# Self-attention and involution on one core: exponentials summed by transposed reductions over pairs of key tiles, three rotating banks of tap weights, and a finer end of the last image

## The chip, the cores and the metric

The kernel runs on one core of one Trainium2 chip. The metric is the device time of one execution in microseconds (us). All data are float32. The engines are TensorE (PE, matmuls; PEld its weight loads), VectorE (DVE), ScalarE (ACT), GpSimd (POOL) and SyncE (SP), whose queue issues nearly all DMAs.

## The reference

The input x has 4 images of 512 channels and 64 x 64 pixels (n = 4096). Two layers follow one another.

```
q, k, v = wq x + bq, wk x + bk, wv x + bv          # 128 channels each
attn    = softmax(q^T k)                           # 4096 x 4096 per image
y       = wo (v attn^T) + bo + x                   # 512 channels

o1  = relu(s1 * (W1 y) + b1)                       # 128 channels
w   = Ws relu(sr * (Wr o1) + br) + bs              # 8 groups x 49 taps per pixel
inv[g,c,h,w] = sum over the 7 x 7 taps of w[g,tap,h,w] * o1_padded[g,c,h+i,w+j]
out = s3 * (W3 inv) + b3 + y
```

The 16 channels of a group share the 49 weights of a pixel.

## The kernel before

The whole program is written out in Python, so that the order in which a function emits instructions is the order on each engine. `fast_path` does the work; a slower `general_path` follows only if a test of the softmax sums fails.

**Attention.** For each image `keys_values` makes the keys `kt` and the values `vT` for 4096 positions. `attention` then goes through 8 blocks of 512 queries (a block is a chunk of 8 image rows); the last block of the last image is cut into two of 256 queries. A block has 32 steps, one for each tile of 128 keys: `score` multiplies keys and queries (`pss`), ACT takes the exponential into `pt` (L665), and PE multiplies it by the values into the bank `po`. Scores run two steps ahead. A block of 256 queries puts two key tiles into one step, so it has 16 steps. The sum of the exponentials over the keys is kept beside it: at each step DVE adds `pt` to an accumulator `pacc` in PSUM (L694 copies the first, L696 adds, L699 adds the last into `sums`). `ptpool` has five buffers, `ps_s` two.

**The end of a block.** `finish_block` is a generator: `chores`, called in each step, advances it a little, so that its matmuls lie between those of the next block. It reduces `sums` in 32 x 32 transposed blocks (L537), adds the four partition groups up by a matmul (`pl`), takes the reciprocal, spreads it, scales `on`, projects (`pwo`, added to x at L560), makes o1 (`p`), writes it to DRAM (`pix`, padded) and makes the reduced channels `red` for the weights. Only one such generator advances at a time.

**Involution.** A unit is 4 image rows (`UR`), so an image has 16 units and a chunk two. A unit holds two tiles (`NT`) of 2 rows x 64 columns = 128 pixels, with pixels on partitions. `weights` multiplies `red` into the taps' weights `pw` of both tiles, in two PSUM banks. `ring` keeps 12 rows (`RING`) of o1 as windows of 7 columns; `pump` loads them from `pix` as rows get written and as older ones come free. For each of the 7 columns x and for two groups of row offsets (`DYS`: 4 and 3), one DVE multiplication (L356) covers both tiles: 4 x 2 x 128 = 1024 elements for the first group, 768 for the second. Where the 12-row ring wraps within a group, each is cut into pieces of 512 and 512, or 512 and 256. Four product buffers (`prods`) lie between DVE and POOL, which adds the products into `acc` (L380) and at the end of the unit adds its four rows up (L389).

The involution is emitted by `pace`, a planner inside `chores`: an instruction is emitted when enough PE time has passed (`TAPS_A_US`), its rows are expected in the ring, and the planned backlog of DVE and POOL is under a few us. A new unit first waits for its predecessor's last planned DVE instruction:

```
yield from until(free["dve"] + 0.3)
pw = early.pop((b, u), None) or weights(b, u)
```

**The tail.** After the last attention matmul the list `tail` is filled and the planner no longer waits: a loop takes one step of `finishing`, one of `closing` and one of the taps in turn. Every second product is then added by PE (`pa`, a matmul with the identity) and not by POOL. `closing` holds `turn_unit`, which brings a unit's sums into channel order, and `close_chunk`, which multiplies by W3 (`py`), adds (L461) and stores. The last chunk closes in two halves of 256 pixels.

PSUM has eight banks: two for `ps`, one each for `po` and `pacc` (tag "acc"), two for `pw` and two for `ps_s`. After the attention the two of `ps_s` go to a second buffer of `pw`.

Of the kernel before, what the change touches and what calls it, by code (L numbers as in the profile page):

```python
# [15 lines left out]
P = 128  # L16
# [44 lines left out]
DYS = (0, 4), (4, 3)  # L61
TAPS_A_US = 1.56

# [4 lines left out]
DVE_OP, POOL_OP = 0.7, 1.28  # L68
# [15 lines left out]
def fast_path(  # L84
# [28 lines left out]
    ptpool = pool("pt", 5)  # L113
# [12 lines left out]
    wpools, early = [ps1], {}  # L126
# [16 lines left out]
    okr = const.tile([P, 1], F32, name="okr")  # L143

# [70 lines left out]
    def v1(i):  # L215
        return vec[:, i : i + 1]
# [23 lines left out]
    def pump():  # L240

        nonlocal load
        while load // STEP in written:
            b, row = divmod(load, STEP)
            rows, us = written[b]

            end = H + SR - UR if rows == H else rows + PAD - 1
            n = min(b * STEP + end, low + RING) - load
            n = min(n, RING - load % RING, PIECE if b == B - 1 else RING)
            if n <= 0:  # L250
                break
            for h in range(2):
                src = pix[b % 2][row + h : row + h + n, :W, :]
                windows = bass.AP(
                    tensor=src.tensor, offset=src.offset, ap=[[P, W], [WP * P, n], [1, K * P]]
                )
                nc.sync.dma_start(
                    ring[h * W : (h + 1) * W, load % RING : load % RING + n]
                    .rearrange("p r x c -> p r (x c)"),
                    windows,  # L260
                )
            free["dma"] = max(free["dma"], us)
            us = takes("dma", ROW_US * n) + LAND_US
            landing.update((load + i, us) for i in range(n))
            load += n
            if row + n == H + SR - UR:
                load = (b + 1) * STEP
# [7 lines left out]
    def weights(b, u):  # L275
        red, col = reds[b, u]
        wpools.append(wpools.pop(0))
        pw = wpools[0].tile([P, NT, CH], F32, tag="w", name=f"pw_{b}_{u}")
        for t in range(NT):

            rows = slice(t * (P // NT), t * (P // NT) + CR + 1)
            pixels = slice(col, col + P)
            mm(
                pw[:, t, : NTAP * G], red[rows, pixels], wt[rows, O_WT : O_WT + NTAP * G],
                shared=2,
            )
        return pw
# [17 lines left out]

    def involution():
        nonlocal low, due
        while True:
            while not units:
                yield "none"  # L310
            b, u = units.pop(0)
            acc = work2.tile([P, NT, 4, P], F32, tag="acc", name=f"acc_{b}_{u}")
            yield from until(free["dve"] + 0.3)
            pw = early.pop((b, u), None) or weights(b, u)
            begin = pe + 0.5
            pa, ops = None, []
            base = b * STEP + u * UR
            for dy0, n in DYS:

                at = (base + dy0) % RING  # L320
                whole = at + n + NT < RING + 1
                pieces = [(dy0, n)] if whole else [(dy0, 2), (dy0 + 2, n - 2)]
                ops += [(x, dy, k) for x in range(K) for dy, k in pieces]
            for o, (x, dy, n) in enumerate(ops):
                if o and dy >= DYS[1][0] > ops[o - 1][1]:
                    low = base + UR
                    pump()
                    if tail and units:
                        early[units[0]] = weights(*units[0])
                rows = [(base + dy + t * 2) % RING for t in range(NT)]  # L330
                while base + dy + n + NT > load:
                    yield "wait"
                landed = max(landing[base + dy + i] for i in range(n + NT))
# [6 lines left out]
                free["pool"] = max(free["pool"], takes("dve", DVE_TAPS[0] + DVE_TAPS[1] * n))  # L340
                takes("pool", POOL_TAPS[0] + POOL_TAPS[1] * n)
                due -= n
                d0 = dy - DYS[dy >= DYS[1][0]][0]
                first = x == 0 and dy < DYS[1][0]
                prod, p0 = acc, d0
                if not first:
                    prod, p0 = prods.tile(
                        [P, NT, 4, P], F32, tag="prod", name=f"prod_{b}_{u}_{o}"
                    ), 0
                col = (x * K + dy) * G  # L350
                lines = ring[:, rows[0] : rows[0] + n, x, :]
                image = bass.AP(
                    tensor=lines.tensor, offset=lines.offset,
                    ap=[lines.ap[0], [(rows[1] - rows[0]) * K * P, NT], [K * P, n], [1, P]],
                )
                product = nc.vector.tensor_tensor(  # L356
                    prod[:, :, p0 : p0 + n, :].rearrange("p t d (g c) -> p t d g c", g=G),
                    image.rearrange("p t d (g c) -> p t d g c", g=G),
                    pw[:, :, col : col + n * G].unsqueeze(3)
                    .broadcast_to([P, NT, n * G, GC])  # L360
                    .rearrange("p t (d g) c -> p t d g c", d=n),
                    ALU.mult,
                )
                if not tail:
                    tc.keep_in_program_order(product)
                if first:
                    pass
                elif tail and o % 2:

                    begun = pa is not None  # L370
                    if not begun:
                        pa = ps1.tile([P, NT, P], F32, tag=("po", "acc")[u % 2], name=f"pa_{b}_{u}")
                    for t in range(NT):
                        for d in range(n):
                            mm(
                                pa[:, t, :], prod[:, t, d, :], ident,
                                not begun and t == d == 0, False,
                            )
                else:
                    nc.gpsimd.tensor_tensor(  # L380
                        acc[:, :, d0 : d0 + n, :], acc[:, :, d0 : d0 + n, :], prod[:, :, :n, :],
                        ALU.add,
                    )
# [89 lines left out]
    def keys_values(b):  # L473
# [3 lines left out]
        for i, c in enumerate(KEYS):  # L477
# [20 lines left out]
            pv = ps1.tile([P, 4, P], F32, tag=("po", "acc")[i % 2], name=f"pv_{b}_{c}")  # L498
# [21 lines left out]
    def finish_block(b, c, off, n, po, sums):  # L520
# [5 lines left out]
        def pause(us, steps):  # L526
# [11 lines left out]
            blocks, sums.rearrange("p (k q) -> p k q", q=TB), AX.X, ALU.add, apply_transpose=True  # L538
# [3 lines left out]
        for i in range(CH // n):  # L542
            mm(pl, quads, blocks[:, i * n // TB : (i + 1) * n // TB], i == 0, i == CH // n - 1)
# [77 lines left out]
        pr = ps.tile([P, CH // NT], F32, tag="mm", name=f"pr_{name}")[:, : n // NT]  # L621
        for t in range(NT):
            half = slice(t * (P // NT), (t + 1) * (P // NT))
            mm(
                pr[half], w_slice(O_WP, 0)[:, half],
                o1.rearrange("p (u t x) -> p u t x", t=NT, x=P)[:, :, t, :], shared=2,
            )
        red = redpool.tile([P, CH // NT], F32, tag="red", name=f"red_{name}")[:, : n // NT]
        nc.scalar.activation(red, pr, AF.Relu, bias=v1(V_BP), scale=v1(V_SP))
        for i in range(tiles // NT):  # L630
            reds[b, top // UR + i] = red, i * P
# [15 lines left out]
    def attention(b, kt, vT, q):  # L647
        blocks = [(c, 0, CH) for c in range(NCH)]
        if b == B - 1:

            blocks[-1:] = [(NCH - 1, off, CH // 2) for off in (0, CH // 2)]

        steps = [(k, j) for k, (_, _, n) in enumerate(blocks) for j in range(N // P * n // CH)]
        qs, pts, pos, paccs = {}, {}, {}, {}
        qs[0] = q

        def score(m):
# [6 lines left out]
            pt = ptpool.tile([P, CH], F32, tag="pt", name=f"pt_{b}_{k}_{j}")  # L664
            nc.scalar.activation(pt, pss, AF.Exp)  # L665
            pts[m] = pt
# [3 lines left out]
        for m, (k, j) in enumerate(steps):  # L670
            c, off, n = blocks[k]
            nj = N // P * n // CH
            if j == 0:
                pos[k] = ps1.tile([P, CH], F32, tag="po", name=f"po_{b}_{k}")[:, :n]
                paccs[k] = ps1.tile([P, CH], F32, tag="acc", name=f"pacc_{b}_{k}")
# [9 lines left out]
            pt = pts.pop(m)  # L685
# [6 lines left out]
            takes("dve", DVE_OP)  # L692
            if j == 0:
                nc.vector.tensor_copy(paccs[k], pt)  # L694
            elif j < nj - 1:
                nc.vector.tensor_tensor(paccs[k], paccs[k], pt, ALU.add)  # L696
            else:
                sums = work1.tile([P, CH], F32, tag="sums", name=f"sums_{b}_{k}")
                nc.vector.tensor_tensor(sums, paccs.pop(k), pt, ALU.add)  # L699
                f = finish_block(b, c, off, n, pos.pop(k), sums)  # L700
                next(f)
                finishing.append(f)
# [17 lines left out]
    wpools.insert(0, pool("ps_w", 1, space=bass.MemoryType.PSUM, reuse_waits="tile"))  # L720
    wpools.reverse()
# [403 lines left out]
```

## Time and profile before

| what | value |
|---|---|
| timed runs, median (lowest to highest of 3) | 2607.41 us (2604.98 to 2607.64) |
| profiled execution, first to last instruction | 2605.7 us |
| median less the span | 1.7 us |
| PE busy | 2587.9 us (99%), granted clock 0.997 |
| DVE busy | 1874.2 us (72%) |
| POOL busy | 1823.5 us (70%) |
| ACT busy | 835.8 us (32%) |
| DMA | 244 MB, 38.6% of 16 engines' span |

The profile was taken in one execution; it gives no time of its own beside the span, so the 1.7 us stand for what lies around it. A "busy" time is the union of an engine's instructions. "Idle before" is the time in which an engine had nothing running before the instructions of that group, and the arrow names what ended it. In a timeline a row is a run of like instructions: start, length, engine, line, operation, tile written and tiles read, shape, count. In the window view a row gives each engine's busy time in that stretch with its number of instructions, then the granted clock of PE, the share of the DMA engines and GB/s. The attention's last matmul starts near 2526 us; the last tap product ends at 2593.3 us.

### The profile page before, as it was taken

The numbers are of one execution on the slowest core, as the hardware profiler recorded it, in microseconds if no ns is written. First come the engines' busy times: TensorE is split into PE (matmuls) and PEld (weight loads), VectorE is DVE, ScalarE is ACT, GpSimd is POOL, SyncE is SP. The second block draws the span as 40 slices with busy tenths as digits, with TensorE's granted clock in tenths as the row PEclk, the third lists the DMA queues.
The fourth block names the chain that finished last, engine by engine and source line by source line (L and its number), as shares of the span: only waits on it lengthen the run. The fifth ranks groups of instructions, "written<-read, shape, count | busy, mean of one in ns | idle before, by whom it ended". The sixth has DMA issues, their size and how long they took to land.

```text
span 2605.7 us, 24569 instructions
## 1 busy us (share of the span) xinstructions
PE 2587.9 (99%) x7484; PEld 1246.5 (48%) x7484; DVE 1874.2 (72%) x2677; ACT 835.8 (32%) x1378; POOL 1823.5 (70%) x1197
## 2 busy tenths in 40 slices
PE   9999999999999999999999999999999999999998
PEld 7444444445544444444644444444464444444577
DVE  0447777877575787788676678788757678777887
ACT  1333333332233333333223333333323333333330
POOL 0007788877881788887885468888788577877886
PEclk9999999999999999999999999999999999999999
DMA  6033232445615344233651434443463433222343
GB/s 236 1 75 63 55 85 73 99 99 150 164 43 112 63 101 95 61 84 82 180 129 45 103 69 101 101 92 74 118 171 83 101 93 93 72 60 58 73 91 102
DMA packets 208798, 244.33 MB, mean 94 GB/s; under 512 B 109640, under 2 KB 128528, under 8 KB 208528
## 3 DMA queue, kind: packets, MB, share of 16 engines
q1 hardware_dynamic: 208224, 242.31, 38.6%
q8 instruction: 61, 1.00, 0.2%
q14 instruction: 81, 0.66, 0.1%
q10 hardware_dynamic: 432, 0.36, 0.0%
HBM read 193.57 MB, written 49.06 MB: 93 GB/s over the span
## 4 chain that ended last, share of the span: by engine, by line
PE 91%; POOL 4%; DVE 3%; issue 1%; DMA 0%; ACT 0%; SPq 0%; POOLq 0%; DVEq 0%; ACTq 0%
PE pss L220 32%; PE po L220 31%; PE pv L220 4%; PE pk L220 4%; PE pq L220 4%; PE pwo L220 4%; PE py L220 4%; PE p L220 4%; POOL acc L380 4%; PE pw L220 2%; DVE prod L356 1%; PE pa L220 1%; DVE pacc L696 1%; PE pr L220 1%; POOL acc L389 0%
## 5 line engine op out<-in xcount | busy, mean ns | idle before, releaser
L380 POOL TENSOR_TENSOR acc<-acc,prod 128x768 f32<-128x768 f32 (+3 forms) x1063 | 1701.5, 1620 | 760.5 <-DVE prod L356 712.4
L220 PE MATMUL pss<-q,k 128*128 128x512 f32 (+1 forms) x2112 | 1056.3, 585 | 0.0
L220 PE MATMUL po<-pt,v 128*128 128x512 f32 (+1 forms) x2112 | 1047.7, 581 | 0.0
L665 ACT ACTIVATE pt<-pss 128x512 f32<-128x512 f32 x1024 | 611.3, 597 | 1252.0 <-PE pss L220 1184.9
L356 DVE TENSOR_TENSOR prod<-ring,pw 128x512 f32<-128x512 f32 (+3 forms) x1092 | 886.7, 847 | 44.6 <-POOL acc L380 41.7
L696 DVE TENSOR_TENSOR pacc<-pacc,pt 128x512 f32<-128x512 f32 x958 | 664.6, 694 | 243.2 <-ACT pt L665 216.2
L220 PEld LDWEIGHTS po<-pt,v 128*128 128x128 f32 x2112 | 399.3, 190 | 482.2 <-issue 462.2
L220 PEld LDWEIGHTS pss<-q,k 128*128 128x128 f32 x2112 | 391.9, 190 | 466.2 <-issue 459.3
L404 DVE STREAM_TRANSPOSE turned<-acc 128x256 f32<-128x256 f32 x48 | 21.4, 446 | 217.4 <-POOL acc L389 217.4
L220 PE MATMUL py<-accT,wt 128*128 128x512 f32 (+1 forms) x264 | 132.3, 584 | 4.0 <-DVE x L461 3.3
L220 PE MATMUL pwo<-on,wt 128*128 128x512 f32 (+1 forms) x264 | 130.3, 586 | 0.0
L220 PEld LDWEIGHTS pv<-wt,x 128*128 128x128 f32 x1024 | 119.6, 192 | 15.3 <-issue 15.0
L389 POOL TENSOR_TENSOR acc<-acc 128x512 f32<-128x512 f32 x120 | 119.5, 996 | 9.4
L461 DVE SCALAR_TENSOR_TENSOR x<-py,vec,x 128x512 f32<-128x512 f32 (+1 forms) x132 | 95.7, 726 | 36.1 <-PE py L220 35.8
L220 PE MATMUL pv<-wt,x 128*128 128x128 f32 x1024 | 120.2, 275 | 0.0
L220 PE MATMUL p<-x,wt 128*128 128x512 f32 (+1 forms) x264 | 119.2, 579 | 0.0
L578 ACT ACTIVATE x<-x,vec 128x512 f32<-128x512 f32 (+1 forms) x132 | 92.9, 706 | 80.0 <-PE p L220 74.9
L220 PE MATMUL pk<-x,wt 128*128 128x512 f32 x256 | 117.3, 596 | 0.1
L220 PE MATMUL pq<-x,wt 128*128 128x512 f32 (+1 forms) x264 | 115.4, 580 | 0.0
L560 DVE SCALAR_TENSOR_TENSOR x<-pwo,bo,x 128x512 f32<-128x512 f32 (+1 forms) x132 | 95.2, 727 | 22.8 <-PE pwo L220 21.7
L356 DVE TENSOR_TENSOR acc<-ring,pw 128x1024 f32<-128x1024 f32 (+1 forms) x84 | 78.7, 955 | 17.6 <-PE pw L220 17.6
L220 PEld LDWEIGHTS pq<-x,wt 128*128 128x128 f32 x264 | 50.0, 190 | 60.2 <-issue 56.7
(57 smaller groups left out, 733.6 us busy)
## 6 DMA issues: line engine op xcount, KB each, us to landing
x<-x_dram SPq DMA_DIRECT2D x55, 1024.0 KB, 5.7
ring<-pix SPq DMA_DIRECT2D x74, 448.0 KB, 8.3
ring<-pix SPq DMA_DIRECT2D x24, 1344.0 KB, 9.7
out_dram<-x SPq DMA_DIRECT2D x31, 1024.0 KB, 4.2
ring<-pix SPq DMA_DIRECT2D x24, 896.0 KB, 10.7
ring<-pix SPq DMA_DIRECT2D x30, 672.0 KB, 10.2
ring<-pix SPq DMA_DIRECT2D x6, 2240.0 KB, 19.5
pix<-o1t SPq DMA_DIRECT2D x192, 32.0 KB, 1.7
```

The source lines that it names most:

```text
L220: return nc.tensor.matmul(o, lhsT=lhsT, rhs=rhs, start=start, stop=stop)
L356: product = nc.vector.tensor_tensor(prod[:, :, p0 : p0 + n, :].rearrange("p t d (g c) -> p t d g c", g=G), image.rearrange("p t d (g c) -> ...
L380: nc.gpsimd.tensor_tensor(acc[:, :, d0 : d0 + n, :], acc[:, :, d0 : d0 + n, :], prod[:, :, :n, :], ALU.add,)
L389: nc.gpsimd.tensor_tensor(acc[:, :, :n, :], acc[:, :, :n, :], acc[:, :, n : 2 * n, :], ALU.add)
L404: nc.vector.transpose(blocks.rearrange("p (t k q) -> p t k q", t=NT, q=TB), acc[:, :, 0, :].rearrange("p t (k q) -> p t k q", q=TB),)
L461: nc.vector.scalar_tensor_tensor(xt[:, t, :], py, v1(V_S3 + t), xt[:, t, :], ALU.mult, ALU.add)
L560: nc.vector.scalar_tensor_tensor(xt[:, t, :], pw, bo[:, t : t + 1], xt[:, t, :], ALU.add, ALU.add)
L578: nc.scalar.activation(xt[:, t, :], xt[:, t, :], AF.Identity, bias=v1(V_B3 + t))
L665: nc.scalar.activation(pt, pss, AF.Exp)
L696: nc.vector.tensor_tensor(paccs[k], paccs[k], pt, ALU.add)
```

## The change

Five things are done at once.

1. `pt` holds a pair of key tiles (three buffers of 2 x 512 and not five of 512). After each second step DVE reduces the pair with a transposed `tensor_reduce` to 32 numbers per partition in `sums`; `finish_block` then adds those up over the pairs with one strided reduction. `pacc` and its PSUM bank go, and `pv` has one bank.
2. The tap weights lie in three PSUM banks that rotate by tile (`taps_w`, `slots`). A unit's second row group is done one tile after the other. While the second tile is done, the next unit's weights are made in the bank that is free and in the one that the first tile has left.
3. The products of a unit's second group have 384 elements and not 768 (or 256 and 128 where the ring wraps, which is now only in the second tile).
4. The last block of the last image is 256, 128 and 128 queries. Its last two units are done in the parts that `LAST` lists (unit, tiles, first row offset, number of offsets), in an order in which some parts of both need no row of the last 128 queries. Two padded rows (`PADDED`) are neither loaded nor multiplied.
5. In the tail the sums on PE (`pa`) have two banks of their own, and weights need none.

```diff
-    ptpool = pool("pt", 5)
+    ptpool = pool("pt", 3)
...
+    taps_w = ps1.tile([P, WSLOTS, CH], F32, tag="w", name="taps_w")
...
+PADDED = 2
+LAST = (
+    (0, (0, 1), 0, 2), (0, (0, 1), 2, 2),
+    (0, (0, 1), 4, 2), (0, (0,), 6, 1), (1, (0,), 0, 4),
+    (0, (1,), 6, 1), (1, (1,), 0, 4), (1, (0, 1), 4, 1), (1, (0,), 5, 2),
+)
...
+    def slots(b, u):
+        first = (b * NU + u) * NT
+        return [(first + t) % WSLOTS for t in range(NT)]
...
-    def weights(b, u):
-        red, col = reds[b, u]
-        wpools.append(wpools.pop(0))
-        pw = wpools[0].tile([P, NT, CH], F32, tag="w", name=f"pw_{b}_{u}")
-        for t in range(NT):
+    def weights(b, u, tiles=range(NT)):
+        for t in tiles:
+            red, col = reds[b, u * NT + t]
+            slot = slots(b, u)[t]
             rows = slice(t * (P // NT), t * (P // NT) + CR + 1)
             pixels = slice(col, col + P)
             mm(
-                pw[:, t, : NTAP * G], red[rows, pixels], wt[rows, O_WT : O_WT + NTAP * G],
-                shared=2,
+                taps_w[:, slot, : NTAP * G], red[rows, pixels],
+                wt[rows, O_WT : O_WT + NTAP * G], shared=2,
             )
...
     def involution():
...
+            if b == B - 1 and u == NU - 2:
+                yield from until(drained + 0.3)
+                yield from last_units(b, u)
+                return
-            yield from until(free["dve"] + 0.3)
-            pw = early.pop((b, u), None) or weights(b, u)
-            begin = pe + 0.5
+            if (b, u) not in early:
+                yield from until(drained + 0.3)
+                weights(b, u)
+            begin = early.pop((b, u), pe) + 0.5
...
+            for tiles, (dy0, n) in ((range(NT), DYS[0]), ((0,), DYS[1]), ((1,), DYS[1])):
+                ops += [(tiles, x, dy, k) for x in range(K) for dy, k in pieces(tiles, dy0, n)]
...
+                if o and tiles[0] > ops[o - 1][0][0]:
+                    drained = free["dve"]
...
+                if tiles[0] and units and units[0] not in early and (tail or pe > drained + 0.3):
+                    weights(*units[0])
+                    early[units[0]] = pe
...
+    def last_units(b, u0):
+        for i, (v, tiles, dy, n) in enumerate(LAST):
+            u = u0 + v
+            while v and not tail:
+                yield "wait"
+            base = b * STEP + u * UR
+            while base + dy + 2 * tiles[-1] + n > load:
+                yield "wait"
...
+            for x in range(K):
...
+                pas[v] = multiply_add(
+                    b, u, accs[v], pas[v], tiles, x, dy, n, f"{i}_{x}",
+                    x == 0 and dy < DYS[1][0], bool(tail) and (x + i) % 2,
+                )
+                yield
+            if ends[v] == i:
+                closing.append(turn_unit(b, u, accs[v], pas[v], takes("pool", POOL_OP * 1.5)))
...
     def finish_block(b, c, off, n, po, parts):
...
         nc.vector.tensor_reduce(
-            blocks, sums.rearrange("p (k q) -> p k q", q=TB), AX.X, ALU.add, apply_transpose=True
+            blocks[:, : n // TB], parts.rearrange("p (j k) -> p k j", k=n // TB), AX.X, ALU.add
         )
...
-        for i in range(CH // n):
-            mm(pl, quads, blocks[:, i * n // TB : (i + 1) * n // TB], i == 0, i == CH // n - 1)
+        mm(pl, quads, blocks[:, : n // TB])
...
-            blocks[-1:] = [(NCH - 1, off, CH // 2) for off in (0, CH // 2)]
+            blocks[-1:] = [(NCH - 1, 0, 2 * P), (NCH - 1, 2 * P, P), (NCH - 1, 3 * P, P)]
...
-            pt = ptpool.tile([P, CH], F32, tag="pt", name=f"pt_{b}_{k}_{j}")
-            nc.scalar.activation(pt, pss, AF.Exp)
-            pts[m] = pt
+            if j % 2 == 0:
+                pts[k, j // 2] = ptpool.tile([P, 2, CH], F32, tag="pt", name=f"pt_{b}_{k}_{j}")
+            nc.scalar.activation(pts[k, j // 2][:, j % 2, :], pss, AF.Exp)
...
-            takes("dve", DVE_OP)
-            if j == 0:
-                nc.vector.tensor_copy(paccs[k], pt)
-            elif j < nj - 1:
-                nc.vector.tensor_tensor(paccs[k], paccs[k], pt, ALU.add)
-            else:
-                sums = work1.tile([P, CH], F32, tag="sums", name=f"sums_{b}_{k}")
-                nc.vector.tensor_tensor(sums, paccs.pop(k), pt, ALU.add)
+            if j % 2:
+                pair = pts.pop((k, j // 2))
+                takes("dve", DVE_PAIR)
+                nc.vector.tensor_reduce(
+                    sums[k][:, (j - 1) * CH // TB : (j + 1) * CH // TB],
+                    pair.rearrange("p i (k q) -> p (i k) q", q=TB),
+                    AX.X, ALU.add, apply_transpose=True,
+                )
```

`multiply_add` is the body of the old loop (the product on DVE, then the sum on POOL or PE), taken out into a function that is given the tiles.

## The prediction, written before the changed kernel was run

> **What bounds the kernel now.** I read the page first, then the window view of the end of the run, the groups kept apart by shape, the waits, and the timeline of the tail.
>
> ```profile
> PE 2587.9 (99%) x7484; PEld 1246.5 (48%) x7484; DVE 1874.2 (72%) x2677; ACT 835.8 (32%) x1378; POOL 1823.5 (70%) x1197
> ```
> PE is full and the others are not. Since a busy PE need not be PE at its best, I looked at starts: from 2480 to 2510 us four 256-column instructions begin every 0.865 us without a hole, at clock 1.00. So up to the attention's end (2526.2 us) the time is the number of PE columns; work taken off DVE or POOL there is worth nothing by itself.
>
> ```profile
> core 0: us, PE busy (x) PEld busy (x) DVE busy (x) ACT busy (x) POOL busy (x), PEclk, DMA share, GB/s
> 2405.00:2477.00 72.00, 72.00 (x228) 39.56 (x228) 57.35 (x79) 27.50 (x47) 59.61 (x38) 1.00 0.30 70
> 2477.00:2526.00 49.00, 49.00 (x232) 41.37 (x229) 39.73 (x59) 18.12 (x34) 39.87 (x27) 1.00 0.48 102
> 2526.00:2541.60 15.60, 12.25 (x55) 9.60 (x54) 12.86 (x21) 2.42 (x6) 11.98 (x7) 0.78 0.26 59
> 2541.60:2556.30 14.70, 14.70 (x118) 12.99 (x119) 12.78 (x19) 1.44 (x4) 9.28 (x6) 1.00 0.80 193
> 2556.30:2577.50 21.20, 20.02 (x136) 16.18 (x136) 20.18 (x32) 0.37 (x1) 15.70 (x13) 1.00 0.45 119
> 2577.50:2593.30 15.80, 14.30 (x116) 13.21 (x115) 15.04 (x18) 0.37 (x1) 13.64 (x8) 1.00 0.08 26
> ```
> The last four rows are the tail up to the last product. DVE is busy 12.86 + 12.78 + 20.18 + 15.04 = 60.9 of 67.3 us: the tail is DVE's, with 6.4 us idle. Then 12.4 us follow to 2605.7 (last sums, `py`, stores).
>
> ```profile
> 2508.43 1.81 POOL L380 TENSOR_TENSOR acc<-acc,prod 128x768 f32<-128x768 f32 x1 [2.62 <-DVE prod L356]
> ...
> 2516.35 9.68 POOL L380 TENSOR_TENSOR acc<-acc,prod 128x1024 f32<-128x1024 f32 x4 [3.95 <-PE pr L220]
> ```
> Between unit 11 and unit 12 POOL stands for 2.6 and 3.95 us: the next unit's weights wait for the last product of the one before.
>
> **The change, part by part.** The sum is made against the span of 2605.7 us; the median of the timed runs is 1.7 us above it, which I leave as it is.
>
> *Sums over pairs.*
> ```profile
> L696 DVE TENSOR_TENSOR pacc<-pacc,pt 128x512 f32<-128x512 f32 x958 | 664.6, 694 | 243.2 <-ACT pt L665 216.2 <-DVE rls L546 0.2
> ...
> L537 DVE TRANSPOSE_TENSOR_REDUCE blocks<-sums 128x16 f32<-128x512 f32 x33 | 23.5, 711 | 1.1
> ```
> Removed: 1024 adds and copies of some 0.69 us and 33 reductions of 0.711, 733 us of DVE. Added: 512 reductions of 1024 elements, and 34 strided ones of up to 512 elements, 23 us at 0.7. The trace has no 1024-element transposed reduction. From below: 0.711 plus 512 elements at the slope of the products (1.209 - 0.679 us for 1024 and 512 elements) is 1.24 us; from above: twice 0.711 is 1.42. I take 1.24, since a longer pattern starts once: 635 + 23 = 658 us, 75 saved; at 1.42, 750 us, 17 lost. Either way nothing on the path: DVE idles 730 us. The Trainium skill, VectorE: DVE Perf Modes, section Rules for kernel authors, speaks against this part: it calls `tensor_reduce` the slowest DVE operation and advises to restructure. By that rule a pair would cost more than two adds (over 1.39 us) and the 75 us would be a loss; by the row, 711 against 694 ns for the same 512 elements, it is a draw per element. No run here has decided that yet.
>
> What can reach PE is the buffer: an exponential waits until DVE has done with an older `pt`.
> ```profile
> ACT pt L665 <- PE pss L220: 1184.9, 932, 4.8
> ...
> ACT pt L665 <- DVE prod L356: 39.0, 31, 2.0
> ...
> ACT pt L665 <- DVE pacc L696: 13.3, 11, 2.0
> ```
> These 42 waits are at most 2.0 us, where ordinary idling before an exponential is 1.13: at most 0.9 us late. A released pair comes 1.24 - 0.69 = 0.55 us later than a released tile, so 1.45. With two score banks PE meets a late exponential only after about 1.8 us (two steps of 1.73 us, less the 0.86 of one score, the 0.6 us exponential and 0.2 to start). Taken at nothing.
>
> *One bank for `pv`, none for `pacc`.* Between two `pv` lie 3.4 us of `pk`, and the copy takes 0.59 us on ACT: nothing.
>
> *Second group by tile.*
> ```profile
> L380 POOL TENSOR_TENSOR acc<-acc,prod 128x768 f32<-128x768 f32 x298 | 540.6, 1814 | 69.6 <-DVE prod L356 48.0
> ...
> L356 DVE TENSOR_TENSOR prod<-ring,pw 128x768 f32<-128x768 f32 x308 | 280.9, 941 | 6.1 <-POOL acc L380 4.9 <-PE pa L220 0.4
> L356 DVE TENSOR_TENSOR prod<-ring,pw 128x512 f32<-128x512 f32 x380 | 248.6, 679 | 28.5 <-POOL acc L380 27.0 <-DMA ring<-pix 1.3
> ...
> L380 POOL TENSOR_TENSOR acc<-acc,prod 128x256 f32<-128x256 f32 x140 | 102.5, 732 | 63.0 <-DVE prod L356 62.8
> ```
> A POOL add of 384 elements lies between 732 and 1278 ns (256 and 512): 1.0 us. Fourteen against seven of 1.814 is +1.3 us per unit, also where the ring wraps (7.0 + 7 x (0.73 + 0.46) against 7 x (1.28 + 0.73)): some 84 us more on POOL, 1907 of 2606, and about 60 us on DVE by the same step. Hidden while a unit gets 36 us (starts at 2408.5, 2438.9, 2477.6, 2513.9) and needs some 32 of POOL.
>
> *Weights ahead.* PE makes the same weights, earlier; the wait before a unit goes. What is late next is POOL. From 2405 to 2526 it idles 121 - 99.5 = 21.5 us; of this some 16 us are gaps at three handovers like the one shown. Less 1.35 us more work for each of 3.5 units (4.7), 11 to 17 us of POOL come free. A unit is some 14.5 us of DVE to 31 of POOL, so 5 to 7.8 us of products are done before the attention ends. More than 7.8 cannot be: that is what is left of unit 12 at 2526.2 (1.6 us, and 7 products of 0.88). I take -6.0; from nothing (the planner's lag stops it) to -7.8.
>
> *The tail's products.*
> ```profile
> 2560.29 4.86 DVE L356 TENSOR_TENSOR prod<-ring,pw 128x512 f32<-128x512 f32 x8
> ...
> 2578.63 4.60 DVE L356 TENSOR_TENSOR prod<-ring,pw 128x1024 f32<-128x1024 f32 x4
> ```
> Back to back a product of 512 takes 0.61 us and one of 1024 1.15, hence 0.88 (768), 0.47 (384), 0.34 (256), 0.20 (128). Unit 13: 7 x (1.15 + 0.61 + 0.34) = 14.7 becomes 7 x (1.15 + 0.47 + 0.34 + 0.20) = 15.1. Unit 14: 7 x (1.22 + 0.88) = 14.7 becomes 21 x 0.61 + 14 x 0.20 = 15.6. Unit 15: 14.2 becomes, without the padded rows, 14 x 0.61 + 14 x 0.34 = 13.3. Sum +0.4.
>
> *Smaller query blocks.* The last 256 queries take 128 instructions of 256 columns in the attention, at 0.216 us; as 256 of 128 columns, at the 0.1115 of `pv` (32 in 3.57 us), 28.5 against 27.6, and a little in the projections: +1.2 on PE. A third `finish_block` adds about 2.2 us of DVE (reciprocal, spread, product, four adds at 0.35), partly before the attention ends: +1.5, between 0 and 2.2. Its DMAs (two to `pix`, the loads of the ring) go past SP, which issues few others there. That the parts in `LAST` need fewer rows saves nothing here: the ring's last loads are issued by 2553 us, and DVE has units 13 and 14 to do until 2577.
>
> *Idle time and end.* Smaller pieces fill some of the 6.4 us: -1, from 0 to -3. PE's last sums waited for a POOL add of 1.81 us; it becomes 0.73: -0.9.
>
> Sum: +1.2 - 6.0 + 0.4 + 1.5 - 1.0 - 0.9 = -4.8, span 2600.9, time 2602.6 us.
>
> **Rivals.**
>
> *A greater gain.* All of unit 12 is done (-7.8), DVE's idling falls to 1 us (-5.4), the third block ends before the attention does (0): -7.8 - 5.4 + 1.2 + 0.4 - 0.9 = -12.5, so 2595. For it: DVE is what the tail waits for. Against: the idling is in ten small waits for `pwo`, `py` and POOL, which remain.
>
> *No gain.* The planner refuses what the earlier weights allow, because its backlog of POOL (1.0 us an instruction, 14 for 7) is at its limit: 0 for unit 12, no less idling, +1.2 + 0.4 + 2.2 - 0.9 = +2.9; if POOL's 4.7 us more also leave 2.3 us of products behind, +5.2: 2610 to 2613. For it: POOL is 82% busy from 2405 on.
>
> *Slower: PE waits for the exponentials.* Place: every second exponential, behind a pair's reduction on DVE. Price: 42 such waits times 0.55 us is 23 us at most, with the gain of the tail 2625; half, 2614. It decides once a pair is released over 0.35 us later than I reckon (1.8 - 1.45), for which a reduction of 1.42 us in a row of them would do. Against: PE has no hole from DVE today.
>
> That the change doesn't do what it says: if DVE instructions behind the pair's reduction are held by late exponentials, weights come early but products don't; that is the second rival.
>
> **How the numbers follow.** Forecast 0.45 (2598 to 2607), greater gain 0.18 (2592 to 2598), no gain 0.21 (2607 to 2613), slower 0.16 (2613 to 2630). A measurement of this kernel can tell about 0.2% (5.2 us) from no change: faster is under 2602.2, slower over 2612.6. The forecast's case splits 0.27 faster and 0.18 the same; with the greater gain 0.45 faster; same 0.18 + 0.18 of the no-gain case; slower 0.16 + 0.03. The range 2593 to 2613 leaves out most of the slower case and the edge of the greater gain.
>
> **What would show it.** In the changed profile: reductions of 1024 elements near 1.24 us; `pss` still without waits; the attention's end near 2527.4; unit 13's first product within 2 us of that; last product near 2589; tail DVE under 5.5 us idle. Wrong if ACT's waits for DVE pass 2.5 us with holes in PE, or if unit 12 still has over 5 us of products at the attention's end.

## The result, and the profile after

The changed kernel takes 2645.43 us (median of 4 runs, 2643.94 to 2646.50), the kernel before 2607.52 beside it: 1.0149 times as long, interval 1.0136 to 1.0162. The forecast was 2602.6, its range 2593 to 2613. The profiled execution spans 2644.7 us.

The page's line of the engines:

```profile
PE 2602.6 (98%) x7576; PEld 1255.3 (47%) x7576; DVE 1878.4 (71%) x2635; ACT 838.5 (32%) x1387; POOL 1904.0 (72%) x1641
```

PE is busy 14.7 us longer (a slower clock counts as busy) and idle 24.3 us longer (2644.7 - 2602.6 = 42.1 us, against 17.8). POOL's total is what the prediction worked out (1907). So POOL's instructions have the expected sizes. The windows, cut at the last attention matmul (2557.8 us, before 2525.9):

```profile
core 0: us, PE busy (x) PEld busy (x) DVE busy (x) ACT busy (x) POOL busy (x), PEclk, DMA share, GB/s
2405.00:2477.00 72.00, 70.33 (x183) 31.98 (x182) 59.01 (x77) 25.18 (x43) 63.53 (x47) 1.00 0.30 70
2477.00:2526.00 49.00, 49.00 (x247) 38.35 (x246) 39.12 (x64) 18.92 (x33) 37.67 (x42) 1.00 0.43 100
...
2557.80:2573.00 15.20, 13.20 (x71) 10.47 (x70) 12.89 (x26) 3.93 (x11) 10.47 (x10) 0.78 0.50 139
2573.00:2589.00 16.00, 12.71 (x81) 9.90 (x80) 10.88 (x24) 0.00 (x0) 11.86 (x12) 0.93 0.40 86
2589.00:2605.00 16.00, 14.80 (x85) 12.21 (x85) 14.21 (x25) 0.37 (x1) 10.85 (x10) 0.86 0.03 13
2605.00:2631.50 26.50, 22.77 (x134) 18.88 (x135) 20.02 (x49) 0.38 (x1) 17.37 (x21) 0.87 0.15 54
```

The loss is in the attention: it ends 31.9 us later, the tail after it is 86.9 us in place of 79.8. In the tail's four rows up to the last product (2631.5) DVE is busy 58.0 of 73.7 us, so it idles 15.7 us where it idled 6.4 before.

What the attention waits for is in the waits (waiting engine and tile, releaser: us in total, times, longest). Of the kernel before:

```profile
DVE turned L404 <- POOL acc L389: 217.4, 48, 7.3
DVE prod L356 <- POOL acc L380: 41.7, 76, 1.8
...
PE py L220 <- DVE x L461: 3.3, 3, 1.1
```

Of the changed one:

```profile
DVE prod L345 <- POOL acc L367: 153.2, 278, 1.9
DVE turned L491 <- POOL acc L476: 79.3, 30, 5.9
ACT pt L758 <- DVE prod L345: 28.1, 24, 2.0
PE taps_w L232 <- DVE prod L345: 22.5, 16, 2.3
DVE prod L345 <- PE taps_w L232: 15.0, 17, 2.0
...
ACT pt L758 <- DVE sums L787: 5.0, 5, 1.3
```

DVE's products wait for POOL's adds 278 times, not 76, and PE, which had three holes of 1.1 us and three of 0.2 in the attention, now has 16 in front of the tap weights there, 22.5 us in all. None stands in front of a score, so the exponentials are not what PE waits for. The timeline shows one such place (start, length, engine; in brackets the idle time before and its releaser):

```profile
2103.48 0.56 DVE L345 TENSOR_TENSOR prod<-ring,taps_w 128x384 f32<-128x384 f32 x1 [0.52 <-POOL acc L367]
2104.55 0.55 DVE L345 TENSOR_TENSOR prod<-ring,taps_w 128x384 f32<-128x384 f32 x1 [0.52 <-POOL acc L367]
...
2105.29 0.60 ACT L758 ACTIVATE pt<-pss 128x512 f32<-128x512 f32 x1 [1.12 <-PE pss L232]
...
2106.70 0.56 DVE L345 TENSOR_TENSOR prod<-ring,taps_w 128x384 f32<-128x384 f32 x1 [0.52 <-POOL acc L367]
...
2107.77 0.56 DVE L345 TENSOR_TENSOR prod<-ring,taps_w 128x384 f32<-128x384 f32 x1 [0.52 <-POOL acc L367]
2108.24 1.24 DVE L787 TRANSPOSE_TENSOR_REDUCE sums<-pt 128x32 f32<-128x1024 f32 x1
2108.38 0.30 PEld L232 LDWEIGHTS taps_w<-wt,red 33*128 33x128 f32 x4 [3.10 <-DVE prod L345]
2108.38 1.23 PE L232 MATMUL taps_w<-wt,red 33*128 33x392 f32 x4 [2.27 <-DVE prod L345]
```

Back to back, DVE starts a product of 384 elements every 0.47 us; here it starts one every 1.07 us, as POOL's adds free the buffers, so all four are taken. The pair's reduction at 2108.24 starts behind the last of these products, though the last exponential before it was done at 2105.89: DVE keeps to the program's order. PE has come to the next unit's weights in its order. They go into the bank which the first tile's seven products read, the last of them ends at 2108.33, and all attention work queued behind on PE has stood for 2.27 us. At 2109 to 2112.5 the granted clock is 0.53.

**Theory A.** The planner lets POOL fall up to 7.5 us behind. Four buffers of 768-element products hold 4 x 1.81 = 7.3 us of POOL's adds; of 384-element products they hold 4 x 1.00 = 4.0. DVE, in order as above, is then held by a product that has no buffer, and whatever is queued behind it is late against the plan by which PE's instructions were placed. Rivals: the weights are made too early (the plan's margin of 0.3 us); the single-tile products cost as such; the pair sums are in the way.

### The profile page after: what moved, and what is told of

It is laid out like the page before. It is cut to its first block, busy times and chain, and to the rows that moved or that the text cites. A ratio compares the mean times of both kernels' runs of the same rounds, so it can differ in the third digit from the quotient of the medians.

```text
span 2644.7 us, 24158 instructions
## 1 busy us (share of the span) xinstructions
PE 2602.6 (98%) x7576; PEld 1255.3 (47%) x7576; DVE 1878.4 (71%) x2635; ACT 838.5 (32%) x1387; POOL 1904.0 (72%) x1641
## 3 DMA queue, kind: packets, MB, share of 16 engines
q1 hardware_dynamic: 207904, 241.39, 37.8%
## 4 chain that ended last, share of the span: by engine, by line
PE 80%; POOL 10%; DVE 5%; issue 2%; DMA 1%; SPq 0%; ACT 0%; POOLq 0%; DVEq 0%; ACTq 0%
PE pss L232 30%; PE po L232 29%; POOL acc L367 10%; PE pq L232 4%; PE py L232 4%; PE p L232 3%; PE pwo L232 3%; DVE prod L345 3%; PE taps_w L232 2%; PE pv L232 2%; PE pk L232 2%; DVE sums L787 1%; PE pa L232 1%; PE pr L232 1%; DMA x<-x_dram 1%
## 5 line engine op out<-in xcount | busy, mean ns | idle before, releaser
L367 POOL TENSOR_TENSOR acc<-acc,prod 128x384 f32<-128x384 f32 (+4 forms) x1507 | 1783.0, 1197 | 718.3 <-DVE prod L345 650.3
L232 PE MATMUL pss<-q,k 128*128 128x512 f32 (+2 forms) x2176 | 1059.2, 574 | 0.0
L345 DVE TENSOR_TENSOR prod<-ring,taps_w 128x384 f32<-128x384 f32 (+4 forms) x1553 | 930.9, 638 | 179.1 <-POOL acc L367 153.2
L232 PE MATMUL po<-pt,v 128*128 128x512 f32 (+2 forms) x2176 | 1049.9, 569 | 0.0
L787 DVE TRANSPOSE_TENSOR_REDUCE sums<-pt 128x32 f32<-128x1024 f32 x512 | 631.0, 1236 | 288.6 <-ACT pt L758 286.7
L232 PE MATMUL pwo<-on,wt 128*128 128x512 f32 (+2 forms) x272 | 129.8, 571 | 0.6 <-DVE on L639 0.6
L232 PE MATMUL p<-x,wt 128*128 128x512 f32 (+2 forms) x272 | 120.4, 572 | 0.0
L664 ACT ACTIVATE x<-x,vec 128x512 f32<-128x512 f32 (+2 forms) x136 | 94.0, 694 | 77.0 <-PE p L232 71.8
L232 PE MATMUL pq<-x,wt 128*128 128x512 f32 (+2 forms) x272 | 115.5, 567 | 0.0
L646 DVE SCALAR_TENSOR_TENSOR x<-pwo,bo,x 128x512 f32<-128x512 f32 (+2 forms) x136 | 94.3, 699 | 15.7 <-PE pwo L232 14.3
L232 PE MATMUL taps_w<-wt,red 33*128 33x392 f32 x256 | 64.3, 551 | 22.5 <-DVE prod L345 22.5
## 6 DMA issues: line engine op xcount, KB each, us to landing
ring<-pix SPq DMA_DIRECT2D x24, 896.0 KB, 10.4
```

The source lines that it names most:

```text
L232: return nc.tensor.matmul(o, lhsT=lhsT, rhs=rhs, start=start, stop=stop)
L345: product = nc.vector.tensor_tensor(prod[:, ts, p0 : p0 + n, :].rearrange("p t d (g c) -> p t d g c", g=G), image.rearrange("p t d (g c) - ...
L367: nc.gpsimd.tensor_tensor(acc[:, ts, d0 : d0 + n, :], acc[:, ts, d0 : d0 + n, :], prod[:, ts, :n, :], ALU.add,)
L646: nc.vector.scalar_tensor_tensor(xt[:, t, :], pw, bo[:, t : t + 1], xt[:, t, :], ALU.add, ALU.add)
L664: nc.scalar.activation(xt[:, t, :], xt[:, t, :], AF.Identity, bias=v1(V_B3 + t))
L787: nc.vector.tensor_reduce(sums[k][:, (j - 1) * CH // TB : (j + 1) * CH // TB], pair.rearrange("p i (k q) -> p (i k) q", q=TB), AX.X, ALU.a ...
```

## The experiments

Each ratio is against runs of the kernel before on the same chip (2606.2 to 2606.8 us).

**1. A wider margin.** At the three places that wait for the predecessor's products:

```diff
-yield from until(drained + 0.3)
+yield from until(drained + 4.3)
```

> The changed kernel, but the next unit's weights are made only when the planned end of the first tile's products is 4.3 us past, not 0.3. Theory A (PE stands in front of taps_w, because products of 384 elements are held at POOL's pace by the four product buffers and end later than planned): the 16 waits of 0.5 to 2.4 us (25 us) nearly go, with them the four stretches at half clock before the tail; the attention ends near 2530 us instead of 2557.8, time near 2618. Theory B (the time is lost to more work or to the pair reductions, whenever the weights are made): attention's end stays within 5 us of 2557.8, time near 2645.

2652.2 us, ratio 1.0180 (1.0163 to 1.0197). PE still stands 30.1 us in 20 holes in front of `taps_w`, and the attention ends at 2566.7 us, where theory A expected 2530 and theory B at most 2562.8. So the margin is no cure, and the expectation of a recovery fell. One reading is that DVE's queue is late and a later place in the plan moves the products behind it too; no run shows that.

**2. Two products to a buffer.** A buffer has room for two tiles, and a single-tile product fills half of it; now the next one takes the other half, so four buffers hold eight. Instructions and their number stay.

```diff
-            prod, p0 = prods.tile([P, NT, 4, P], ...), 0
+            if nt == 1 and half:
+                prod, ps_ = half.pop(), slice(1, 2)
+            else:
+                prod = prods.tile([P, NT, 4, P], ...)
+                half.clear()
+                if nt == 1:
+                    half.append(prod)
+                    ps_ = slice(0, 1)
```

> The changed kernel, but two single-tile products share one product buffer, so that eight of them and not four can lie between DVE and POOL; weights are made when the planner says, as in the changed kernel. Theory A: DVE's waits for POOL fall from 153 us to under 50, PE's waits for taps_w from 22 us (in the list of waits) to under 6, attention's end near 2533, time near 2620. If the planner's 0.3 us are too short for another reason (finish_block's and the pair reductions' DVE work), PE still waits over 15 us and the attention ends after 2548.

2607.66 us, ratio 1.0004 (0.9995 to 1.0014): 37.8 us come back, where theory A expected some 25. The waits (it expected under 50 in the first row):

```profile
DVE prod L355 <- POOL acc L377: 61.2, 85, 2.1
DVE prod L355 <- PE taps_w L232: 28.1, 22, 3.1
```

PE has no hole left in the attention, which ends at 2526.6 us. POOL is as busy as in the changed kernel (1906.1 us). So, with the weights made ahead, neither POOL's larger work nor the single-tile products as such cost the 38 us; the room did. Experiment 9 shows that room is not enough when the weights come at the end. The tail is 79.3 us, so what the change was to gain there does not come.

**3. Weights made at the end, as before, buffers as changed.** Until the tail, a unit's weights are made after its predecessor's last product.

```diff
-                if o and tiles[0] > ops[o - 1][0][0]:
-                    drained = free["dve"]
...
-                if tiles[0] and units and units[0] not in early and (tail or pe > drained + 0.3):
+                if tail and tiles[0] and units and units[0] not in early:
...
+            drained = free["dve"]
             low = max(low, (b + 1) * STEP if u == NU - 1 else base + UR)
```

> The changed kernel, but until the tail the weights of a unit are made when its predecessor's last planned product is over, as in the kernel before; the products by tile stay. Theory A as told (early weights are what PE meets): waits for taps_w under 6 us, attention's end near 2530. If small products alone are enough (the unit's last products are held by POOL just as the first tile's are): PE waits as often, 64 times up to 2 us, attention's end at 2550 or later.

2665.69 us, ratio 1.0223 (1.0206 to 1.0240): worse, as the rival had it. The 37.6 us of holes now stand in front of `py`, `taps_w`, `pl`, `pq` and `pwo`. The early weights were only the first to meet the late DVE; anything that PE needs of DVE will do.

**4. The pair sums alone, in the kernel before.** The lines of point 1 of the change, of which these are the core; all else is as before.

```diff
-                nc.vector.tensor_tensor(paccs[k], paccs[k], pt, ALU.add)
+            if j % 2:
+                nc.vector.tensor_reduce(
+                    sums[k][:, (j - 1) * CH // TB : (j + 1) * CH // TB],
+                    pair.rearrange("p i (k q) -> p (i k) q", q=TB), ...
```

> The kernel before with the pair sums alone (three pairs of pt, transposed reductions of 1024 elements, strided reduction at the block's end). Theory A: nothing on PE, attention's end 2526 within 1.5 us, time 2607 within 4. The rival of the prediction (exponentials wait for a pair's reduction and PE for them): holes in PE before pss and po, time 2614 to 2630.

2602.90 us, ratio 0.9985 (0.9975 to 0.9995). The rival of slower exponentials is out: alone this part gains 3.8 us. The attention ends at 2524.1 us, 1.8 earlier, the tail is 2.6 shorter, and DVE is busy 1823.6 us, 50.6 less. Theory A's "nothing on PE" missed by a little: PE's holes behind DVE in the attention fall from 4.0 to 2.2 us, and the one stretch at half clock in the attention (383.2 to 386.6 us in the kernel before) does not occur.

**5. Two product buffers in the kernel before.** Nothing else is touched.

```diff
-    prods = pool("prods", 4)
+    prods = pool("prods", 2)
```

> The kernel before, untouched but for its product buffers: two in place of four. Theory A (a product on VectorE waits for a buffer that GpSimd's add has not yet emptied; the buffers hold less GpSimd work than the planner's 7.5 us of backlog): two buffers with 768-element products hold 2 x 1.81 = 3.6 us, somewhat less than the 4 x 1.00 us of the changed kernel, so this kernel must lose about as much or more: VectorE's waits for GpSimd in front of products from 41.7 us to 150 us or more, holes on TensorE, the attention's end at 2555 to 2580, time 2640 to 2670 us. Rival B (the loss comes with the single-tile products themselves: more instructions, more releases): none of that here, 2606 to 2613 us.

2730.61 us, ratio 1.0480 (1.0464 to 1.0496), a loss far above the 2640 to 2670 us that theory A gave, while rival B's 2606 to 2613 is out:

```profile
DVE prod L356 <- POOL acc L380: 314.6, 469, 1.7
...
PE pw L220 <- DVE prod L356: 32.6, 12, 4.1
```

The old kernel without room does what the changed one does, and PE stands in front of the old weights `pw`.

**6. A shorter backlog,** in the changed kernel.

```diff
-POOL_LAG = 4.0, 7.5
+POOL_LAG = 4.0, 4.0
```

> The changed kernel with the planner's limit on GpSimd's backlog in the attention lowered from 7.5 to 4.0 us, so that it plans no more than the four buffers hold (4 x 1.00 us). Theory A: VectorE is no longer held; its waits for GpSimd in front of products fall from 153 to 40 to 80 us, TensorE's holes before the tap weights go, the attention ends at 2525 to 2532; GpSimd may run dry at times and units start later, so the tail may take 80 to 88 us: 2607 to 2620 us. Rival C (GpSimd simply hasn't the time for fourteen adds in place of seven, whatever the planner lets through): the time stays at 2635 to 2655 us.

2644.71 us, ratio 1.0145 (1.0130 to 1.0161): a miss. The attention ends 11.4 us earlier than in the changed kernel, the tail is 10.4 us longer. DVE is still held for 126.0 us. The time lies where rival C put it, but kernel 2 makes the same adds on POOL in 2607.7 us, so the adds alone are not the cause. The limit is tested before an add is planned, so 4.0 lets 5.0 us through, more than the buffers' 4.0. That cannot be the whole reason: counted the same way, 7.5 lets 9.3 through in the kernel before, whose buffers hold 7.3, and there it costs next to nothing. How the planner's limit enters is not shown. POOL running dry would lengthen the tail; that too was not tried.

**7 and 8. The end of the last image,** both with two products to a buffer. In 7 the end is as before: all three edits below; in 8 only the last of them, so the parts stay.

```diff
-PADDED = 2
+PADDED = 0
...
-            if b == B - 1 and u == NU - 2:
-                yield from until(drained + 0.3)
-                yield from last_units(b, u)
-                return
...
-            blocks[-1:] = [(NCH - 1, 0, 2 * P), (NCH - 1, 2 * P, P), (NCH - 1, 3 * P, P)]
+            blocks[-1:] = [(NCH - 1, off, CH // 2) for off in (0, CH // 2)]
```

> The changed kernel with two single-tile products to a buffer, and the end of the last image as in the kernel before: two blocks of 256 queries, whole units, the padded rows. Theory D (the new end of the last image gives nothing; what it saves it pays back in a third finishing block, single-column products and TensorE's smaller blocks): attention's end 2524 to 2526, tail 77 to 80, time 2602 to 2606 us, 2 to 5 below the 2607.7 with the new end. Rival E (the new end is worth the 4.8 us of the forecast, and the weights made ahead or the shared buffers cost as much elsewhere): 2609 to 2614 us.

> The changed kernel with two single-tile products to a buffer, its parts of units kept, but the last 512 queries as two blocks of 256, not 256 + 128 + 128. By the terms on record TensorE saves 1.2 us and the third finishing block 1.5 us: 2605 us against 2607.7. Theory F (the small blocks are what gives the parts something to do early): the parts wait for the last 256 queries' rows, 2610 to 2618 us.

7: 2603.14 us, ratio 0.9988 (0.9979 to 0.9997). 8: 2605.40 us, ratio 0.9996 (0.9987 to 1.0005). So theory D holds: the small blocks cost 2.3 us (2607.66 - 2605.40; 1.8 when each is taken against the kernel before on its own chip) and the parts another 2.3. In the tail of 8 DVE idles 10.4 us before its last product, in 7 5.7. DVE's timeline in 8 shows where:

```profile
2570.63 0.29 DVE L355 TENSOR_TENSOR prod<-ring,taps_w 128x128 f32<-128x128 f32 x1 [0.47 <-POOL acc L377]
2572.35 0.69 DVE L355 TENSOR_TENSOR acc<-ring,taps_w 128x512 f32<-128x512 f32 x1 [1.43 <-PE taps_w L232]
2572.96 4.66 DVE L355 TENSOR_TENSOR prod<-ring,taps_w 128x512 f32<-128x512 f32 x11
2578.60 0.48 DVE L355 TENSOR_TENSOR prod<-ring,taps_w 128x128 f32<-128x128 f32 x2 [0.98 <-POOL acc L377]
2580.51 0.69 DVE L355 TENSOR_TENSOR acc<-ring,taps_w 128x512 f32<-128x512 f32 x1 [1.43 <-PE taps_w L232]
```

The last unit's two tiles start with weights made on the spot, 1.43 us of DVE each; the third bank doesn't help there.

**9. Room, and weights at the end.** Kernel 7 with the diff of experiment 3.

> Two single-tile products to a buffer, the last image's end as before, and until the tail a unit's weights made when the unit before has issued its last product, not after the first tile's products. By the forecast's term for weights ahead (6.0 us, 0 to 7.8) the 2603.1 us with them ahead become 2606 to 2611 us, unit 12 starts 2 us or more later than at 2501.4, and the tail grows from 75.8 to 79 or more. Rival I (the term is near nothing, since the products issued behind the early weights wait for them on VectorE, 1.3 us in the middle): 2602 to 2605 us, unit 12 within 2 us.

2639.61 us, ratio 1.0128 (1.0113 to 1.0144). Both expectations missed: with products by tile the early weights are worth 36.5 us; in the profiled executions 22.8 of them lie in the attention (its end 2546.9 against 2524.1) and 12.1 in the tail. Its waits, and one place in its timeline:

```profile
DVE turned L496 <- POOL acc L481: 238.6, 48, 9.0
PE pq L232 <- DVE x L553: 12.7, 6, 2.3
PE pl L232 <- DVE blocks L629: 5.6, 4, 2.3
```

```profile
532.77 0.45 DVE L496 STREAM_TRANSPOSE turned<-acc 128x256 f32<-128x256 f32 x1 [6.67 <-POOL acc L481]
533.13 1.20 DVE L792 TRANSPOSE_TENSOR_REDUCE sums<-pt 128x32 f32<-128x1024 f32 x1
...
534.26 0.71 DVE L553 SCALAR_TENSOR_TENSOR x<-py,vec,x 128x512 f32<-128x512 f32 x1
...
535.02 1.63 PE L232 MATMUL pq<-x,wt 128*128 128x512 f32 x2 [2.31 <-DVE x L553]
```

`turned` is the transposition that ends a unit; DVE stands there until POOL has folded the unit's sums: 6.67 us in this place. The `x` behind it reads `py`, which shares its two PSUM banks with the next queries `pq`, and PE stands for 2.31 us. The wait is 100.3 us in kernel 7, 238.6 here, and 217.4 in the kernel before, where it cost nothing that PE shows. So this kernel has room for 8.0 us of adds and still loses 33 us, and most of its holes come behind `turned`: with products by tile and the weights at the end, room alone is not enough. Part of what experiment 3 lost may lie here too.

**10 and 11. The room in steps.** `pool("prods", 5)` in the changed kernel (one product each); `pool("prods", 3)` in the kernel before.

> The changed kernel with five product buffers in place of four, one product to each. Theory A (what counts is how many us of GpSimd's adds the buffers hold): 5 x 1.00 = 5.0 us in the second groups, against 4.0 (2645.4 us) and 8.0 (2607.7 us): between them, attention's end 2532 to 2548, VectorE's waits for GpSimd in front of products 80 to 125 us, time 2613 to 2633 us. Rival G (the shared buffers cured something else than the room): 2640 us or more.

> The kernel before with three product buffers: 3 x 1.81 = 5.4 us of second-group adds. Theory A in us of work: like five buffers in the changed kernel, 2612 to 2640 us, VectorE's waits for GpSimd 90 to 160 us. Rival H (the number of buffers counts, not the us they hold: four single-tile buffers cost 38 us, two double ones 124, so three cost more than four single-tile ones): 2655 to 2690 us.

10: 2622.14 us, ratio 1.0055 (1.0040 to 1.0070). 11: 2627.90 us, ratio 1.0080 (1.0065 to 1.0096). Both fall where theory A put them. Six kernels together, by what the buffers hold of the second group's adds (holes: PE's waits for DVE):

| kernel | buffers hold (us of POOL) | DVE waits for POOL before products (us) | PE holes in the attention (us) | attention ends | time |
|---|---|---|---|---|---|
| 5: before, 2 buffers | 2 x 1.81 = 3.6 | 314.6 | 66.2 | 2621.6 | 2730.6 |
| changed, 4 | 4 x 1.00 = 4.0 | 153.2 | 22.5 | 2557.8 | 2645.4 |
| 10: changed, 5 | 5.0 | 100.1 | 10.6 | 2540.1 | 2622.1 |
| 11: before, 3 | 5.4 | 137.0 | 10.0 | 2539.9 | 2627.9 |
| before, 4 | 7.3 | 41.7 | 4.0 | 2525.9 | 2607.5 |
| 2: changed, shared | 8.0 | 61.2 | 0 | 2526.6 | 2607.7 |

The loss goes with the us of POOL that the buffers hold rather than with their number: three double ones cost less than four single ones. The order is not exact: kernel 11 holds a little more than 10, ends its attention at the same time, and is 5.8 us slower in all. Kernel 9, with its weights at the end, does not fit the table. The step from 4.0 to 3.6 is steeper than the rest; with two buffers DVE can be one product ahead of POOL at most, which may be why.

**12. The last unit's weights in one go.** Kernel 8, both tiles' weights ahead of the unit's first part.

```diff
             fresh = [t for t in tiles if (v, t) not in weighed]
+            if fresh and v:
+                fresh = [t for t in range(NT) if (b, u * NT + t) in reds]
```

> Two single-tile products to a buffer, two last blocks of 256 queries, parts of units kept, but the last unit's weights for both tiles made in one go ahead of its first part, not each tile's ahead of the part that first reads it. If the parts' cost in the tail (80.1 against 75.8 us) is the round trips VectorE - TensorE - VectorE in front of them (two idle stretches of 1.43 us at 2570.9 and 2579.1, and the smaller one of 0.98 beside them), one of them goes: 1.4 to 2.4 us less, 2603.0 to 2604.0 us, VectorE's idle time before the last product 8 to 9 us in place of 10.4. Rival J (the idle time is the order of the parts, and moves to the next product): 2605 us or more.

2603.77 us, ratio 0.9992 (0.9983 to 1.0001), 1.6 us less, and DVE idles 7.8 us in place of 10.4. One of the two waits of 1.43 is gone; the 0.98 us in front of products of 128 elements are 1.22.

## Why the prediction was wrong, step by step

The steps add up by the medians (us): pair sums alone -3.8 (4); tap products by tile with weights ahead, given room, +0.2 (7 against 4); the parts +2.3 (8 against 7); the small blocks +2.3 (2 against 8); the missing room +37.8 (changed against 2). Each step starts where the one before it ends, so that they add up proves nothing; measured are 37.9 to 38.7 in all, by which runs of the kernel before are taken. The steps depend on their order: with the weights at the end (9 against 4) the products by tile cost 36.7. Between 4 and 7 and between 8 and 2 the chip changes; against the kernel before on the same chip these two steps are +0.7 and +1.8.

- **"Second group by tile", "hidden while a unit gets 36 us": this step failed.** Its sizes were right: the add of 384 takes 0.999 us (1.0), POOL in all 1904 (1907). What hides the extra POOL time is the backlog, and the backlog lies in the product buffers. The same cut nearly halves what they hold, from 7.3 to 4.0 us. The sum had no such term; it is 37.8 us. That `DVE prod <- POOL acc` was already 41.7 us in the kernel before stood in the profile, but its size alone was no warning: kernel 4 has 72.1 us of it and is faster.
- **"Weights ahead ... What is late next is POOL": wrong on what follows.** Not POOL itself came late but what stands behind it: DVE, held in order, and then PE, in order too, at the bank the first tile has to leave. The holes of 22.5 us, and four stretches of some 3.4 us at half clock after holes of 1.8 to 2.3 us (about 1.7 us lost in each, 6.8), make 29.3 of the 31.2 us by which the attention ends later than in kernel 2, which differs in the buffers alone.
- **Its -6.0 us.** With room (kernel 7) the tail is 75.9 us, 1.3 shorter than with pair sums alone (77.2), for a forecast of 6.0. Unit 12 does start earlier, at 2501.4 us against 2513.9 before and 2509.6 in kernel 4, but some 3.5 us of its products (seven of 384 elements at 0.47) are left at the attention's end, where the forecast left 1.8. Unit 13 then starts 8.7 us after that end, 3.8 sooner than in kernel 4 (12.5), and by the last product only 0.8 of this remains (63.6 against 64.4): DVE waits for the next unit's weights in the middle of the unit at hand, 1.90 us at 2546.87 and 1.43 here:

```profile
2566.88 0.93 PE L232 MATMUL taps_w<-wt,red 33*128 33x392 f32 x4
2567.85 3.34 DVE L355 TENSOR_TENSOR prod<-ring,taps_w 128x384 f32<-128x384 f32 x7 [1.43 <-PE taps_w L232]
...
2571.11 1.21 DVE L355 TENSOR_TENSOR acc<-ring,taps_w 128x1024 f32<-128x1024 f32 x1
```

  The seven products at 2567.85 are unit 14's second tile; they don't read the weights just made (unit 15's, first used at 2571.11), yet wait for them, presumably because the three banks are one tile of the program. In kernel 7 there are 23 such waits, 29.4 us, before products in all. Against the weights at the end (9) the same step is worth 36.5 us, so in this kernel it pays what the single-tile products cost (36.7), and no more.
- **"The tail's products" and "idle time and end", -1.5 in all: wrong sign.** The parts cost 2.3 us. Smaller pieces did not fill the idle time; they added waits, for weights made on the spot above all.
- **"Smaller query blocks", +1.2 and +1.5: right.** 2.3 measured, or 1.8 as above.
- **"Sums over pairs": right in size, gain missed.** Read 1.24, measured:

```profile
L787 DVE TRANSPOSE_TENSOR_REDUCE sums<-pt 128x32 f32<-128x1024 f32 x512 | 631.0, 1236 | 288.6 <-ACT pt L758 286.7
...
L624 DVE TENSOR_REDUCE blocks<-sums 128x16 f32<-128x512 f32 x31 | 31.7, 1023 | 0.8
```

  The strided reduction takes 1.02 us and not 0.7. By the lines of kernel 4 some 70 us of DVE are saved (forecast 75), 50.6 in its busy total. The step was "taken at nothing" since DVE idled anyway and "PE has no hole from DVE today". That was misread: the waits of the kernel before have `PE py <- DVE x`, 3.3 us, and each of these three holes lies behind products held by POOL and three adds to `pacc` in a row. In kernel 4 this wait is 1.7 us. That the shorter tail comes from DVE's smaller load is argued, not tried. On the Trainium skill's rule (VectorE: DVE Perf Modes, Rules for kernel authors: `tensor_reduce` on a hot path is the slowest DVE operation, restructure): the runs disagree for this form, as a pair costs 1.236 us against two adds of 0.694.
- **The rivals.** "Slower" held 0.16, up to 2630 us, and named the exponentials behind a pair's reduction. ACT's waits for DVE products and sums are 28.1 + 5.0 us, and no score was late: the side was right, the mechanism not. "No gain" had the planner's backlog of POOL at its limit, but let the planner, not the buffers, be what stops, and priced it at 5.2 us at most.

Two versions beat both kernels: 4 (0.9985) and 7 (0.9988); nothing here tells them apart. Open are why a wider margin made it worse (1) and why a shorter backlog made it no better (6).

## What to carry to other kernels

A buffer between two engines that work in order holds so many microseconds of the slower one: when an instruction is cut in two, ask what the buffers hold afterwards. Here the cut took it from 7.3 to 4.0 us and cost 38 us, and two products to a buffer took all of that back, with the weights made ahead. An engine with 30% idle time is not free: price what stands behind it in its queue, and the next engine that needs one of those. A small wait between engines shows where two of them already meet, but its sum doesn't say what it costs (41.7 us before, 72.1 in the faster kernel 4): look for the instructions behind it that a third engine needs.

## What the hardware did that was not expected

- Short holes were followed by a slow stretch of the clock, though not always. After 2.27 us, with matmuls on both sides, the granted clock was 0.5 for some 3.4 us, and the same after holes of 2.13, 1.78 and 2.15 us in the changed kernel, but not after the one of 2.12 us at 1341.7 us. Before the change it came once, from 383.2 to 386.6 us, with no longer hole ahead of it than 1.1 us; two more holes of that length had none behind them. The Trainium skill, TensorE: Matmul & The Clock Gate, section Why this matters for your kernels, advises no gaps over some 3 us; the holes here are all shorter, so keeping to that advice was not enough in these runs.
- A strided `tensor_reduce` of 512 elements took 1.02 us, a transposed one over blocks of the same size 0.71.
